# A four-layer graph network on one core: the last norm of six batches on another path, and the first loads in another order

## The chip, the cores and the metric

The kernel runs on one core of a Trainium2 chip. The metric is the device time of one execution in microseconds, from the runs shown below; lower is better. A profile of one execution goes with it. In the profile PE is TensorE's matmul, PEld its weight load, DVE is VectorE, ACT is ScalarE, POOL is GpSimd, and SP is the engine that issues most DMAs.

## What is computed

The input x has 64 batches of 256 nodes with 128 channels, all float32, and one adjacency matrix adj of 256 x 256 is shared by all batches. Four layers follow one another, each of the form x = layernorm(x + f(x)):

```python
def _layernorm(x, axis=-1, eps=1e-5):
    m = jnp.mean(x, axis=axis, keepdims=True)
    v = jnp.var(x, axis=axis, keepdims=True)
    return (x - m) / jnp.sqrt(v + eps)
...
x = _layernorm(x + _L0_gnn_ref(x, adj, adj, L0_gnn_weight_1), axis=-1)
x = _layernorm(x + _L1_gnn_ref(x, adj, L1_gnn_weight, L1_gnn_bias), axis=-1)
x = _layernorm(x + _L2_gnn_ref(x, adj, L2_gnn_W, L2_gnn_b), axis=-1)
x = _layernorm(x + _L3_gnn_ref(x, adj, adj, L3_gnn_w3_w, ...), axis=-1)
```

Layer 0 propagates x up to three times through adj, with a weight of 128 x 128 for each of seven terms. Layers 1 and 2 propagate once and multiply by one weight. Layer 3 is a gated unit that runs five steps on a state h:

```python
def step(h, _):
    m_in = jnp.einsum('nm,bmd->bnd', in_matrix, h)
    m_out = jnp.einsum('nm,bmd->bnd', out_matrix, h)
    av = jnp.concatenate([m_in, m_out], axis=-1)
    u3 = h @ u3_w.T + u3_b
    z = jax.nn.sigmoid(av @ w3_w.T + w3_b + u3)
    r = jax.nn.sigmoid(av @ w4_w.T + w4_b + u3)
    hv = jnp.tanh(av @ w5_w.T + w5_b + (r * h @ u5_w.T + u5_b))
    h = (1.0 - z) * h + z * hv
    return (h, None)
```

## The kernel before

The 64 batches are worked off in 32 groups of two batches. A group's state is a tile of 128 x 512: two batches times two halves of the nodes, each 128 x 128 and called a q. At most ten groups are in work at once (ACTIVE).

**The order is planned.** The kernel's code does not issue anything directly. Each operation is recorded with an engine, an estimated cost, a lag until its result is seen, and a rank (Plan.add, L61). Plan.order (L84) then simulates the engines with these estimates: at each step it takes the operation that can start earliest, and among those that can start equally early the one with the lowest rank, then the one recorded first. The result is one list, and each engine works off its part of it strictly in order, waiting for whatever the real data needs. The argument `after` of an operation delays it in the plan only. Buffers are slots in pools ("bank" for the eight PSUM banks, "w" for general 128 x 512 tiles in SBUF and so on; L203), and the plan takes into account when a slot comes free.

**Ranks.** Operations of the preamble have ranks written out by hand in calls of `pre`, `fetch` and `load`. A group's operations have the number of the group as rank. Only for the last seven groups (LEVEL) is it different: there each group lies 0.1 above the one before it, and each operation 0.02 above the group's preceding one (Group.rank, L454), so that these groups advance side by side. The load of x of a group has the group's rank less 1.5.

**The preamble** (L232 to L412). POOL builds the identity matrix, TensorE makes 14 transposes of it to warm up (WARM), and SP loads adj (a_nat), x of the first two groups, layer 0's weight w0 (448 KB; w_raw in the profile), then w1 and six raw weights of layers 2 and 3. POOL loads the biases: b1 and b2, spread over all partitions, into two of the three parts of a tile wb (w1 is the third), and six small ones into braw. TensorE transposes adj and squares it. VectorE makes the degree sums of adj (degree, L325), of which POOL takes the power -1/2 (dinv, L342). VectorE makes the sums of w0's parts (w0_sums, L286) and subtracts each row's mean (centre, L295), and does the same to wb (L375), so that layers 0 to 2 deliver results whose mean over the channels is zero already. It forms four sets of block sums of the adjacency matrices (block_sums, L350), with which `propagate` needs seven block products in place of eight. `less` (L386) is the identity with 1/128 subtracted everywhere, that is I - 1/C. The function `transposed` (L389) turns the raw weights on TensorE.

**Layer 3 and the end of a group** (L795 to L827). Layer 3 works on the transposed state hT, with the channels on the partitions. A step propagates h, and makes the products pr and ph in PSUM, from which ScalarE makes r, z and hv; VectorE makes rh, d = hv - hT, e = z*d and the new hT = hT + e. After the last step the result must be turned back, added to y, which is the result of layer 2, and normalised:

- In all groups but the last two, hT is turned back by a VectorE transpose of 32 x 32 blocks and two passes through DRAM (`turned`, `brought`: one DMA out, four back). Then VectorE makes s = hn + y (residual, L539) and its statistics (L480: bn_stats, bn_aggr, variance + eps, negated mean), POOL the power -1/2 and the product with the mean, and ScalarE the scaled and shifted result (L549).
- In the last two groups (END = 4 batches, from batch 60 on), VectorE writes hT in another order, TensorE transposes it (`transposes`, pth, L659), VectorE adds y from there and makes statistics, POOL makes the power, and VectorE itself makes the result (near, L552).

In layers 0 to 2 the sum has the mean zero by construction, so `spread_of` (L507) needs only the squares, which ScalarE sums with accum_out; POOL adds eps and takes the power -1/2.

Of the kernel before, what the change touches and what calls it, by code (L numbers as in the profile page):

```python
# [10 lines left out]
OP = mybir.AluOpType  # L11
# [7 lines left out]
PLAIN = 0  # L19
END = 4  # L20
STEPS = 5
WARM = 14
ONES = (0, 0)
# [134 lines left out]
def kernel(  # L158
# [39 lines left out]
    def mm(o, lhsT, rhs, start, stop, shared=False):  # L198
# [3 lines left out]
              "ve": [P, Q], "rs": [P, Q]}  # L202
    slots = {"bank": BANKS, "x": ACTIVE + 3, "w": 64, "th": 10, "q": 10, "dram1": 8, "dram2": 16, "st": 12, "mv": 12, "ve": 24, "rs": 12}  # L203
    plan = Plan(slots)
# [9 lines left out]

    def pre(rank, engine, cost, run, reads=(), writes=(), lag=None, joint=False):
        lag = lag or {"SP": 2300, "PE": 260, "DVE": 260, "ACT": 130, "POOL": 100}[engine]
        plan.add(engine, cost, lag, rank, run, reads, writes, joint=joint)


    QUEUES = {"SP": (nc.sync, 450), "ACT": (nc.scalar, 450), "POOL": (nc.gpsimd, 1000)}  # L220

    def fetch(rank, o, src, v, queue):
        e, cost = QUEUES[queue]
        pre(rank, queue, cost, lambda: e.dma_start(o, src), [], [v], lag=3000, joint=True)

# [55 lines left out]

    w0_raw = load(0.01, "w0_raw", [P, C, K0], w0)

# [86 lines left out]

    wb, wbm = constant("wb", [P, 3, C]), constant("wbm", [P, 3])
    fetch(0.1, wb.ap[:, 0, :], w1, wb, "SP")
    for i, b in ((1, b1), (2, b2)):
        fetch(0.1, wb.ap[:, i, :], bass.AP(tensor=b.tensor, offset=b.offset, ap=[[0, P], [1, C]]), wb, "POOL")
    pre(0.35, "DVE", 1100, lambda: centre(wb, wbm), [wb], [wb, wbm])  # L375
    w1c, b1c, b2c = ((wb, wb.ap[:, i, :]) for i in range(3))
    raw = {name: load(0.1, f"raw_{name}", [P, src.shape[1]], src, False, "SP")
           for name, src in (("w2", w2), ("w4", w4_w), ("w3", w3_w), ("w5", w5_w), ("u3", u3_w), ("u5", u5_w))}
# [10 lines left out]
    def transposed(name, *parts_):  # L389
        ps, v = temp(f"p_{name}"), constant(name, [P, len(parts_) * P])  # L390

        def run():
            for i, src in enumerate(parts_):
                if src is raw["w2"]:
                    mm(ps.ap[:, i * P:(i + 1) * P], src.ap, less.ap, True, True)
                else:
                    nc.tensor.transpose(ps.ap[:, i * P:(i + 1) * P], src.ap, ident)

        n = len(parts_) * P
        pre(0.4, "PE", len(parts_) * 110, run, [*parts_, less], [ps])  # L400
        pre(0.4, "ACT", act_cost(n), lambda: nc.scalar.copy(v.ap, ps.ap[:, :n]), [ps], [v])
        return [(v, v.ap[:, i * P:(i + 1) * P]) for i in range(len(parts_))]
# [6 lines left out]
    for i, src in enumerate((w3_b, w4_b, w5_b, u3_b, u3_b, u5_b)):  # L409
        fetch(0.2, braw.ap[:, i:i + 1], src.rearrange("(p o) -> p o", o=1), braw, "POOL")  # L410
    pre(0.4, "DVE", 150, lambda: nc.vector.tensor_add(bsum.ap, braw.ap[:, :3], braw.ap[:, 3:]), [braw], [bsum])
# [26 lines left out]
    class Group:  # L438
        def __init__(self, start, nb):
# [3 lines left out]
            self.q, self.width = nb * T, nb * N  # L443

        def view(self, ap):
            return ap[self.start:self.start + self.nb].rearrange("b (t p) c -> p (b t) c", p=P)
# [11 lines left out]
        def add(self, engine, cost, lag, run, reads=(), writes=(), joint=False, behind=()):  # L458
            after = behind if self.first else self.gate
            self.count += 1  # L460
            op = plan.add(engine, cost, lag, self.rank(), run, reads, writes, after, joint)
            self.first = self.first or op
            self.last = op
            return op
# [14 lines left out]

        def statistics(self, tag, s, near):  # L480
            st, mv, ve, rs, nm = (self.val(k, n + tag) for k, n in (
                ("st", "st"), ("mv", "mv"), ("ve", "ve"), ("rs", "rs"), ("ve", "nm")))
            kept = () if near else (nm,)

            def stats():
                for q in range(self.q):
                    nc.vector.bn_stats(st.ap[:, q * 6:(q + 1) * 6], nat(s)[:, q, :])  # L487

            def aggr():
                for q in range(self.q):  # L490
                    nc.vector.bn_aggr(mv.ap[:, 2 * q:2 * q + 2], st.ap[:, q * 6:(q + 1) * 6])
                mean, var = (mv.ap.rearrange("p (q k) -> p k q", k=2)[:, k] for k in range(2))
                nc.vector.tensor_scalar(ve.ap, var, EPS, None, op0=OP.add)
                if not near:
                    nc.vector.tensor_scalar(nm.ap, mean, -1.0, None, op0=OP.mult)

            def scales():
                nc.gpsimd.tensor_tensor(rs.ap, ve.ap, half[:, :self.q], op=OP.pow)
                if not near:
                    nc.gpsimd.tensor_tensor(mv.ap[:, :self.q], nm.ap, rs.ap, op=OP.mult)  # L500

            self.dve(stats, [s], [st], 195 * self.q)
            self.dve(aggr, [st], [mv, ve, *kept], 67 * self.q + (142 if near else 240))
            self.add("POOL", 1010 if near else 1300, 100, scales, [ve, *kept], [rs] if near else [rs, mv])
            return mv, rs
# [33 lines left out]
        def residual(self, tag, ps, resid, left=lambda v: v.ap, right=lambda v: v.ap):  # L539
            s = self.val("w", "s" + tag)  # L540
            self.dve(lambda: nc.vector.tensor_add(right(s), left(ps), right(resid)), [ps, resid], [s])  # L541
            return (s, *self.statistics(tag, s, self.start >= B - END))

        def normalise(self, tag, s, mv, rs):
# [6 lines left out]

            def near():  # L552
                for q in range(self.q):
                    nc.vector.tensor_scalar(nat(y)[:, q, :], nat(s)[:, q, :], mv.ap[:, 2 * q:2 * q + 1],  # L554
                                            rs.ap[:, q:q + 1], op0=OP.subtract, op1=OP.mult)

            if self.start >= B - END:
                self.dve(near, [s, mv, rs], [y], 257 * self.q)
            else:
                self.act(run, [s, mv, rs], [y], 390 * self.q)  # L560
            return y

# [154 lines left out]
        def record(self):  # L717
# [80 lines left out]
            for s in range(STEPS):  # L798
# [3 lines left out]
                self.product(pr, u3T, hT, False, True)  # L802
                r = self.gate_(f"r{s}", pr, AF.Sigmoid, rb)
                rh = self.tensor(f"rh{s}", OP.mult, r, hT)
                ph = self.val("bank", f"ph{s}")
# [5 lines left out]

                d = self.tensor(f"d{s}", OP.subtract, hv, hT)
                e = self.tensor(f"e{s}", OP.mult, z, d, into=pr)
                if s < STEPS - 1:
# [7 lines left out]
            else:  # L822
                hT = self.tensor("hT", OP.add, hT, e, lambda v: v.ap.rearrange("p (k q i) -> p q k i", k=4, q=self.q),
                                 lambda v: v.ap.rearrange("p (q k i) -> p q k i", k=4, q=self.q))
                last = self.residual("3", self.transposes("h", hT), y)
            o = self.normalise("3", *last)
# [67 lines left out]
```

## Time and profile before

| | |
|---|---|
| median of 7 runs | 1358.71 us (1356.84 to 1359.73) |
| the profiled execution's own time | 1358.96 us |
| its span, first to last instruction | 1357.2 us |
| TensorE busy | 1332.8 us, 98% of the span |
| VectorE, ScalarE, POOL busy | 954.1, 755.9, 675.5 us |
| granted TensorE clock, mean | 0.995 of full speed |
| load of w_raw, issue to landing | 7.5 us, issued at 2.27 us |
| last product of layer 3 starts | 1339.04 us |
| last VectorE instruction ends | 1353.19 us |

The page gives busy times by engine, a line of digits for the granted clock in 40 slices, and groups of instructions. The chain of waits follows the execution back from its end, at each step to what released it. Timeline lines give the start, the duration, the engine, the line of the kernel, the operation and its tiles, and in brackets how long the engine was idle before and what ended that. Names are those of the tiles, without the numbers at their ends, so w0_raw is w_raw. A matmul in float32 of 128 x 128 by 128 x 512 is two records; a transpose is one.

### The profile page before, as it was taken

To read this page: it belongs to the slowest core of one execution; us is meant where nothing else is said; L and a number is where in the kernel's file an instruction comes from. 1 tells how busy PE (TensorE), PEld (TensorE's weight loads), DVE (VectorE), ACT (ScalarE), POOL (GpSimd) and SP (SyncE) were. 2 spreads that over 40 slices of the span, in tenths; PEclk is the share of its full clock that TensorE was granted. 3 is DMA by queue.
4 is the path that set the end of the run, shared out by engine and by line. 5 is a ranking of instruction groups with operands and counts; after the bars stand their busy time and mean duration, and the time that the engine had idled before them with its cause. 6 is when DMAs were issued, how large, how long until landed. Compare 5 with 4: busy or idle time off the path is not lost.

```text
span 1357.2 us, 21892 instructions
## 1 busy us (share of the span) xinstructions
PE 1332.8 (98%) x6509; PEld 923.8 (68%) x6509; DVE 954.1 (70%) x2343; ACT 755.9 (56%) x2398; POOL 675.5 (50%) x1095
## 2 busy tenths in 40 slices
PE   8999999999999999999999999999999999999995
PEld 7986666766776776776676667766776776556552
DVE  5356678778667677677767767766565778777778
ACT  4666464665456565657455466554655686444444
POOL 5786343654446544547354455543744685232322
PEclk9999999999999999999999999999999999999998
DMA  6322333433333322434243333332432233333333
GB/s 172 103 63 63 99 96 104 138 109 116 94 102 95 109 72 85 125 109 125 61 126 110 101 102 109 99 99 68 117 94 63 71 102 119 92 101 93 93 91 104
DMA packets 270214, 135.47 MB, mean 100 GB/s; under 512 B 175856, under 2 KB 241648, under 8 KB 270096
## 3 DMA queue, kind: packets, MB, share of 16 engines
q1 hardware_dynamic: 269840, 133.95, 34.0%
q8 instruction: 52, 0.85, 0.3%
q14 instruction: 66, 0.54, 0.1%
q0 software_dynamic: 256, 0.13, 0.1%
HBM read 67.57 MB, written 66.06 MB: 98 GB/s over the span
## 4 chain that ended last, share of the span: by engine, by line
PE 94%; DVE 3%; DMA 1%; issue 1%; ACT 0%; SPq 0%; POOL 0%; POOLq 0%; DVEq 0%; ACTq 0%
PE pr L199 30%; PE ph L199 20%; PE pmg L199 18%; PE py L199 16%; PE pm L199 7%; PE pmq L199 3%; DMA x<-in_x_dram 1%; DMA w_raw<-in_L_gnn_weight_dram 1%; DVE st L487 0%; DVE s L541 0%; DVE rh L714 0%; ACT y L529 0%; DVE y L554 0%; DVE d L714 0%; DVE hT L714 0%
## 5 line engine op out<-in xcount | busy, mean ns | idle before, releaser
L199 PE MATMUL pr<-mg,w435u5T 128*128 128x512 f32 x640 | 320.2, 593 | 0.8 <-ACT r L707 0.8
L599 POOL TENSOR_TENSOR tsg<-h 128x256 f32<-128x256 f32 x128 | 95.2, 743 | 212.1 <-DMA h<-dh 153.8
L707 ACT ACTIVATE r<-pr,bsum 128x512 f32<-128x512 f32 x160 | 109.7, 686 | 151.2 <-PE pr L199 149.6
L714 DVE TENSOR_TENSOR rh<-r,hT 128x512 f32<-128x512 f32 x160 | 126.8, 794 | 71.7 <-ACT r L707 67.5
L707 ACT ACTIVATE pr<-pr,bsum 128x512 f32<-128x512 f32 x160 | 105.6, 660 | 120.7 <-PE pr L199 116.0
L199 PE MATMUL ph<-rh,w435u5T 128*128 128x512 f32 x320 | 164.1, 596 | 0.8 <-DVE rh L714 0.7
L714 DVE TENSOR_TENSOR d<-ph,hT 128x512 f32<-128x512 f32 x160 | 109.8, 686 | 78.0 <-ACT ph L707 77.0
L199 PE MATMUL ph<-mg,w435u5T 128*128 128x512 f32 x320 | 163.4, 593 | 0.0
L199 PE MATMUL pr<-hT,w2u3T 128*128 128x512 f32 x320 | 162.2, 593 | 0.0
L199 PEld LDWEIGHTS pr<-mg,w435u5T 128*128 128x128 f32 x640 | 109.0, 191 | 64.8 <-issue 48.8
L707 ACT ACTIVATE ph<-ph,bsum 128x512 f32<-128x512 f32 x160 | 105.5, 659 | 63.6 <-PE ph L199 63.4
L529 ACT ACTIVATE y<-s,rs 128x128 f32<-128x128 f32 x384 | 122.1, 392 | 15.2 <-POOL rs L518 14.4
L517 POOL TENSOR_SCALAR ve<-ve 128x4 f32<-128x4 f32 x96 | 22.3, 232 | 214.3 <-ACT y L513 214.2
L199 PEld LDWEIGHTS pmg<-s_aTp,tsg 128*128 128x128 f32 x768 | 102.1, 191 | 34.6 <-issue 29.8
L513 ACT ACTIVATE y<-s 128x128 f32<-128x128 f32 x384 | 113.7, 300 | 18.4 <-DVE s L536 18.2
L199 PEld LDWEIGHTS pmg<-aTp,h 128*128 128x128 f32 x512 | 88.0, 197 | 46.8 <-issue 35.4
L714 DVE TENSOR_TENSOR pr<-pr,d 128x512 f32<-128x512 f32 x160 | 110.6, 692 | 1.5
L714 DVE TENSOR_TENSOR hT<-hT,pr 128x512 f32<-128x512 f32 x160 | 108.6, 680 | 1.7
L627 DVE TENSOR_TENSOR usg<-usg,pmg 128x128 f32<-128x128 f32 x160 | 45.2, 284 | 90.9 <-PE pmg L199 67.1
L199 PE MATMUL pmg<-s_aTp,tsg 128*128 128x128 f32 x768 | 106.4, 275 | 0.0
L637 DVE TENSOR_TENSOR mg<-pmg,usg 128x256 f32<-128x256 f32 x160 | 67.1, 420 | 51.9 <-PE pmg L199 50.1
L518 POOL TENSOR_TENSOR rs<-ve,half 128x4 f32<-128x4 f32 x96 | 99.5, 1037 | 8.0
(175 smaller groups left out, 2808.4 us busy)
## 6 DMA issues: line engine op xcount, KB each, us to landing
dh<-th SPq DMA_DIRECT2D x160, 256.0 KB, 2.0
h<-dh SPq DMA_DIRECT2D x256, 128.0 KB, 2.5
x<-in_x_dram SPq DMA_DIRECT2D x32, 256.0 KB, 3.3
hT<-dh SPq DMA_DIRECT2D x128, 64.0 KB, 2.0
out_dram<-y SPq DMA_DIRECT2D x32, 256.0 KB, 2.3
dx<-tx SPq DMA_DIRECT2D x30, 256.0 KB, 2.7
xT<-dx SPq DMA_DIRECT2D x60, 128.0 KB, 2.6
dn<-tn SPq DMA_DIRECT2D x30, 256.0 KB, 2.0
```

The source lines that it names most:

```text
L199: nc.tensor.matmul(o, lhsT, rhs, start=start, stop=stop, skip_group_check=shared)
L513: nc.scalar.activation(nat(y)[:, q, :], nat(s)[:, q, :], AF.Square, scale=C ** -0.5, accum_out=ve.ap[:, q:q + 1])
L517: nc.gpsimd.tensor_scalar(ve.ap, ve.ap, EPS, None, op0=OP.add)
L518: nc.gpsimd.tensor_tensor(rs.ap, ve.ap, half[:, :self.q], op=OP.pow)
L529: nc.scalar.mul(nat(y)[:, q, :], nat(s)[:, q, :], rs.ap[:, q:q + 1])
L599: nc.gpsimd.tensor_tensor(ts.ap[:, :2 * P].rearrange("p (x c) -> p x c", x=2), ins(h)[:, 1], ins(h)[:, :, 0], op=OP.subtract)
L627: nc.vector.tensor_tensor(row(u, 0), row(u, 1), row(ps, 3), op=OP.add)
L637: nc.vector.tensor_tensor(o(m, slice(1, 3)), o(ps, slice(1, 3), False), both, op=OP.add)
L707: self.act(lambda: nc.scalar.activation(t.ap, ps.ap, func, bias=bias[1], scale=1.0), [ps, bias[0]], [t], act_cost(self.width) + 100)
L714: self.dve(lambda: nc.vector.tensor_tensor(out(t), way(a), way(b), op=op), [a, b], [t])
```

## The change

**Layer 3's norm, in the last six batches** (END = 6, so three groups in place of two). The old path of those groups is gone, and with it the cases for `near` in `statistics` and `normalise`. The sum y + h + e is now formed by TensorE in one PSUM bank: hT before the last update, copied by ScalarE into another order (hc), is multiplied by `less`, y by the identity, and e by `less`. A product of the transposed tile with I - 1/C turns it back and subtracts the mean in one; y has the mean zero already. The first two products may run before the last step's e is known; they are held back in the plan until the gate r of the last step. Then ScalarE sums squares, POOL makes the power -1/2, and VectorE multiplies by it. The last hT = hT + e is not formed in these groups.

**The head.** A new copy on VectorE (`made`) writes a few values of the identity into the part of wb that the bias loads overwrite, so that these must wait for it. The six small bias loads are planned after the last of them has landed. w0's load has the rank -1 in place of 0.01, between those of x of the first and the second group. w1 and the raw weights have 0.6 in place of 0.1, the centring of wb 0.9 in place of 0.35, after w0s, and the transposes of the raw weights 2.1 in place of 0.4. There are 12 warming transposes in place of 14, and 48 buffers of kind w in place of 64.

```diff
-END = 4
+END = 6
-WARM = 14
+WARM = 12
...
-    slots = {"bank": BANKS, "x": ACTIVE + 3, "w": 64, ...
+    slots = {"bank": BANKS, "x": ACTIVE + 3, "w": 48, ...
...
-    w0_raw = load(0.01, "w0_raw", [P, C, K0], w0)
+    w0_raw = load(-1, "w0_raw", [P, C, K0], w0)
...
-    fetch(0.1, wb.ap[:, 0, :], w1, wb, "SP")
+
+    made = pre(-9, "DVE", 100, lambda: nc.vector.tensor_copy(wb.ap[:, 1:3, 0], ident[:, :2]), [], [wb])
+    fetch(0.6, wb.ap[:, 0, :], w1, wb, "SP")
     for i, b in ((1, b1), (2, b2)):
-        fetch(0.1, wb.ap[:, i, :], bass.AP(...), wb, "POOL")
-    pre(0.35, "DVE", 1100, lambda: centre(wb, wbm), [wb], [wb, wbm])
+        last = fetch(0.1, wb.ap[:, i, :], bass.AP(...), wb, "POOL", (made,))
+    pre(0.9, "DVE", 1100, lambda: centre(wb, wbm), [wb, w0s], [wb, wbm])
-    raw = {name: load(0.1, f"raw_{name}", [P, src.shape[1]], src, False, "SP")
+    raw = {name: load(0.6, f"raw_{name}", [P, src.shape[1]], src, False, "SP")
...
-        pre(0.4, "PE", len(parts_) * 110, run, [*parts_, less], [ps])
-        pre(0.4, "ACT", act_cost(n), lambda: nc.scalar.copy(v.ap, ps.ap[:, :n]), [ps], [v])
+        pre(2.1, "PE", len(parts_) * 110, run, [*parts_, less], [ps])
+        pre(2.1, "ACT", act_cost(n), lambda: nc.scalar.copy(v.ap, ps.ap[:, :n]), [ps], [v])
...
-        fetch(0.2, braw.ap[:, i:i + 1], src.rearrange("(p o) -> p o", o=1), braw, "POOL")
+        fetch(0.2, braw.ap[:, i:i + 1], src.rearrange("(p o) -> p o", o=1), braw, "POOL", (last,))
...
+        def closing(self, y, hT, e, behind):
+            s, hc = self.val("bank", "s3"), self.val("w", "hc")
+            way, out_ = self.by_tile
+            self.act(lambda: nc.scalar.copy(out_(hc), way(hT)), [hT], [hc])
+
+            def turned(v, start, stop):
+                for q in range(self.q):
+                    mm(s.ap[:, q * P:(q + 1) * P], v.ap[:, q * P:(q + 1) * P], less.ap, start and q == 0, stop, shared=True)
+
+            def early():
+                turned(hc, True, False)
+                mm(s.ap, ident, y.ap, False, False, shared=True)
+
+            self.pe(pe_cost(P, self.q) + pe_cost(self.width), early, [hc, y, less], [s], behind=(behind,))
+            self.pe(pe_cost(P, self.q), lambda: turned(e, False, True), [e, less], [s])
+            o, rs = self.spread_of("3", s)
+            self.dve(lambda: nc.vector.tensor_tensor(nat(o), nat(s), rs.ap[:, :, None].to_broadcast([P, self.q, C]),
+                                                     op=OP.mult), [s, rs], [o])
+            return o
...
                 r = self.gate_(f"r{s}", pr, AF.Sigmoid, rb)
+                gated = self.last
...
                 d = self.tensor(f"d{s}", OP.subtract, hv, hT)
+                if s == STEPS - 1 and self.start >= B - END:
+                    e = self.tensor("e", OP.mult, z, d, *self.by_tile)
+                    break
                 e = self.tensor(f"e{s}", OP.mult, z, d, into=pr)
...
             else:
-                hT = self.tensor("hT", OP.add, hT, e, ...)
-                last = self.residual("3", self.transposes("h", hT), y)
+                o = self.closing(y, hT, e, gated)
+                self.add("SP", 450, 2700, lambda: nc.sync.dma_start(self.view(out), nat(o)), [o], [])
+                return
```

## The prediction

> **What bounds the kernel now.** I read the page first: the busy table and the slices.
>
> ```profile
> PE 1332.8 (98%) x6509; PEld 923.8 (68%) x6509; DVE 954.1 (70%) x2343; ACT 755.9 (56%) x2398; POOL 675.5 (50%) x1095
> ...
> PEclk9999999999999999999999999999999999999998
> ```
>
> TensorE is busy in 98% of the span, at full clock. By the windows it is idle for about 2.2 us in all between 40 and 1330 us. So only three things can move the time: how early this saturated stretch starts, how much work is put into it, and how long the tail behind it is. For the start I read the chain of waits of the first 60 us.
>
> ```profile
> 2.27 7.54 DMA w_raw<-in_L_gnn_weight_dram
> 9.84 0.39 DVE w0s L287
> ...
> 21.73 0.63 DVE tx L730
> ...
> 29.43 4.71 DMA x<-in_x_dram
> 34.28 0.68 PE pmq L199 x4
> ```
>
> See what leads to what: layer 0's weight w_raw lands at 9.8 us, VectorE works off the whole preamble in one unbroken run until it comes to tx at 21.7, tx releases the stores and, queued behind them on SP, the next loads of x, and TensorE stands until x is there at 34.28. Before w_raw, VectorE sits idle 4.57 us. For the end I read the windows (columns: busy of PE, PEld, DVE, ACT, POOL, then clock, DMA) and the timeline.
>
> ```profile
> 1330.00:1340.00 10.00, 9.00 (x23) 3.44 (x21) 9.37 (x31) 5.44 (x10) 2.89 (x4) 1.00 0.40 127
> 1340.00:1350.00 10.00, 1.94 (x9) 1.13 (x8) 9.83 (x43) 3.84 (x9) 3.35 (x5) 0.80 0.34 97
> ```
>
> ```profile
> 1339.04 1.13 PE L199 MATMUL ph<-rh,w435u5T 128*128 128x512 f32 x2 [0.23 <-DVE rh L714]
> ...
> 1341.72 0.63 ACT L707 ACTIVATE ph<-ph,bsum 128x512 f32<-128x512 f32 x1
> ...
> 1343.67 0.67 DVE L714 TENSOR_TENSOR d<-ph,hT 128x512 f32<-128x512 f32 x1
> ...
> 1344.74 0.69 DVE L714 TENSOR_TENSOR pr<-pr,d 128x512 f32<-128x512 f32 x1
> ...
> 1348.89 0.69 DVE L541 TENSOR_TENSOR s<-pth,y 128x512 f32<-128x512 f32 x1
> ...
> 1352.08 1.11 DVE L554 TENSOR_SCALAR y<-s,mv,rs 128x128 f32<-128x128 f32 x4 [1.12 <-POOL rs L498]
> ```
>
> The last product of the last group starts at 1339.04. From there to the end of its y at 1353.19 there are 14.15 us, and VectorE, 98% busy between 1340 and 1350, is what the group waits for: tanh ends at 1342.35, and d starts only at 1343.67, e at 1344.74, s at 1348.89. In 1330 to 1340 TensorE is still nearly full; the holes the timeline names late in it are 0.78 us (until r of the last group, 1337.69) and 0.23 us (before the line shown).
>
> **What the Trainium skill says here.** "DMA: Bandwidth & Descriptors", Queues, rings and completion order: within one ring descriptors are consumed in order, and a DMA engine takes turns between queues. The trace agrees: the rate falls from 299 GB/s (3 to 4 us) to 153 and 175 GB/s (4 to 6 us) while POOL's bias loads are in flight beside SP's queue. "Perfetto Trace Analysis", Transposes: transposes skip the arithmetic and should not be ordinary matmuls. Here four transposes of pth are four records, while each 128x128 product is two; the change replaces the former by the latter. "ScalarE: Activation LUTs", What ACT_TABLE_LOAD costs: an ACTIVATE with immediate scale takes 186 ns plus 0.833 ns per element, 293 ns for 128; the trace has 298 for the squares at L513. "TensorE: Matmul & The Clock Gate", Part 1: half clock after an idle window; the 0.80 in the window from 1340 agrees.
>
> **Part 1, the head.** *w_raw goes ahead of the second load of x.* 256 KB leave its way; at the 182 GB/s that moved in the window from 0 to 10 us, that is 1.4 us. That it is issued at 1.73 in place of 2.27 is part of those 1.4, not more. *The identity.* Now POOL starts a bias load at 1.28 ahead of the identity's second half (2.15 to 2.46). With the new copy into wb the two bias loads must wait for the identity, so they start about 0.7 us later (identity done near 1.3, copy and hand-off to about 2.0), and six tiny bias loads go behind dinv. Behind the bias loads' new wait on POOL stands only dinv, whose sums end at 5.27: 0. That is a further small relief for w_raw: at least 0, at most some 2 us (half rate for 4 to 6 us, plus what follows); I take 0.3. So w_raw lands near 8.1, 1.7 us earlier. *Centring of wb (1.29 us from 11.03) goes behind w0s.* VectorE's sum stays the same; w0s is ready earlier, which TensorE can use for groups 0 and 1, but it then only waits longer for x at 34.28: 0. If that wait were gone, it would be worth up to the 1.6 us that p_w2u3T now waits on raw weights (0.36 and 1.24). *Two warming transposes fewer* (0.2 us each) and the earlier identity: adjacency ready about 1.5 us sooner, 0 for the same reason. *Raw weights, w1, transposes to later ranks*: SP still has nothing else ready, so I keep their issue times; the transposes (0.9 us of TensorE) only move later, and layers 2 and 3, which use them, start after 40 us: 0. They set a limit: the last lands near 12.5 (where TensorE's wait for raw_u ends), and VectorE reads the group at 14.36. VectorE's run can move forward by at most about 1.9 us before it waits there. Moving 1.7 gives no new wait, and tx, the stores, the x loads and 34.28 all follow. **Head: -1.7**, from 0 to -3.5.
>
> **Part 2, the middle.** Buffers of kind w fall from 64 to 48, and the whole order is computed anew. No row shows a wait for these buffers. Bounds: -2.2 (all idle time between 40 and 1330 gone) to +2 (as much again); I take 0.
>
> **Part 3, the tail, per group of two batches, now three groups.** Removed from VectorE in each of the last two: hT 0.69, s 0.68, four stats 0.87, aggregates 0.37, ve 0.17, y 1.11 = 3.89. Added: o, a 512-wide tensor_tensor from PSUM, 0.69 by the row of d. The third from last loses hT, transpose, s, stats, aggregates, ve and nm, 3.6, for 0.69, and five DMAs on SP. VectorE sheds 3.2 + 3.2 + 2.9 = 9.3 of the 21.2 us it is busy after 1330, and stops being the tail's bound.
>
> Next is the chain of the last group, from its last product: product 1.13, tanh 0.66, d 0.69, e 0.69, four 128x128 products of e (8 records at 0.11 and 0.2 to finish) 1.1, four squares 1.28 (24.43 to 25.71 in group 0), POOL's add and pow 1.35 (26.63 to 27.98), o 0.69, six hand-offs of 0.05: 7.9 us in place of 14.15, **6.25 less**. Squares from PSUM are not shown before; copies of 128 from PSUM at L640 take 0.27, so I see no surcharge (up to 0.2).
>
> But TensorE pays. Four products of h (0.89) and the identity product of y (0.86) are 1.75 per group, products of e 0.89 more: 2.64 against the 0.44 of the transposes. For the groups before the last this comes where TensorE is full. Their ranks: each group lies 0.1 apart, each operation adds 0.02, so the third-last group's closing (2.64) stands ahead of the last group's w5 and later products, and the second-last's (2.64) is tied with the last one. I count 2 x 2.64 = 5.3 ahead of the last product, less the holes of 0.78 and 0.23 and a little of the wait for r at 1331.9 (0.4): **+3.9**. The last group's own 1.75 fits between its last product and e (0.66 + 0.69 + 0.69 with hand-offs: 2.2), nobody waits; if not, it costs up to 1.75. ScalarE's three copies hc (0.59) run before, beside products: 0; y of an older group (1.65) stood ahead of tanh at 1340.16, but with the product 3.9 later it is done. **Tail: -6.25 + 3.9 = -2.3**, from +1 to -5.
>
> **Sum.** -1.7 - 2.3 = -4.0. The profiled run took 1358.96 with a span of 1357.2; less 4.0 it is 1354.96, and the median lies 0.25 under that run: **1354.7 us**.
>
> **Rivals.** *Covers hold:* TensorE's closing work falls into waits for r and rh, only 1.75 of it ahead of the last product (tail -4.5), and w_raw is clear of the bias loads, with the raw weights landing earlier too (head -3.0): -7.5, 1351.2. For it: 4.57 us of idle VectorE before w_raw; against: the raw weights at 12.5. *Given back:* raw weights or x land as late as now (head 0) and the tail keeps 1.0: 1357.7. The change not doing what it says comes to this: were the bias loads not held by the identity, only 1.4 of the head would stay. *Slower, TensorE pays for the tail:* the last group's own 1.75 is also queued ahead of its last product: 7.1 us of matmuls with no hole filled, last product at 1346.1, then tanh behind a 1.65 us normalisation and the pow behind another's 1.35: 7.1 + 3.0 - 6.25 = +3.9, with the head +2.2: 1360.9. It decides where added matmuls and queueing exceed 6.25 + 1.7 = 7.95 us. For it: 9.00 of 10 busy; against: holes exist and ranks put the last closing last.
>
> **Chances.** Forecast 0.50 (own range 1352.5 to 1356.8), covers hold 0.24, given back 0.14, slower 0.12. Range: 1350.4 to 1358.4, which cuts the far halves of the first and the last rival. A measurement here can tell about 0.2% (2.7 us) from none: faster 0.72 (most of the forecast and the first rival), same 0.17, slower 0.11.
>
> **What would show it.** w_raw landing near 8.1, tx at about 20.0, the wait on x ending near 32.6 instead of 34.28; the last ph<-rh product about 2.2 us later than now (1341.2, head included); from its start to the end of o about 7.9 us; o about 0.69. Wrong if VectorE still queues d or e for over 1 us, if tx does not move, or if TensorE's idle time between 40 and 1330 grows beyond 4 us.

## The result and the profile after

The changed kernel takes 1354.27 us (median of 14 runs, 1350.91 to 1355.53), the kernel before, measured beside it, 1358.68 us (34 runs, 1356.39 to 1360.19). The ratio is 0.9967, with a 95% interval of 0.9960 to 0.9974: about 4.5 us faster. The profiled execution of the changed kernel took 1354.07 us with a span of 1352.1, 5.1 less than the 1357.2 of before.

The busy table and the slices of the page after:

```profile
PE 1336.5 (99%) x6553; PEld 928.4 (69%) x6553; DVE 942.2 (70%) x2304; ACT 758.0 (56%) x2421; POOL 679.8 (50%) x1097
...
PEclk9999999999999999999999999999999999999999
```

TensorE has 44 records more and is 3.7 us longer busy, VectorE has 39 instructions fewer and is 11.9 us less busy. The span still is TensorE's.

The start, in the chain that ended last (start, duration, what):

```profile
1.74 8.34 DMA w_raw<-in_L_gnn_weight_dram
...
10.10 0.38 DVE w0s L287
...
36.15 4.32 DMA x<-in_x_dram
40.49 0.71 DVE tx L745
```

w_raw is issued 0.53 us earlier than before (1.74 in place of 2.27), but it takes 8.34 us in place of 7.54, and lands 0.27 later, at 10.08. VectorE's timeline shows the rest:

```profile
10.10 0.38 DVE L287 TENSOR_TENSOR w0s<-w_raw,ident 128x128 f32<-128x128 f32 x1 [4.83 <-DMA w_raw<-in_L_gnn_weight_dram]
...
22.53 0.71 DVE L745 STREAM_TRANSPOSE tx<-x 128x512 f32<-128x512 f32 x1
```

It still stands 4.83 us idle before w_raw (before: 4.57), and tx comes at 22.53, where the chain of before had it at 21.73. So w_raw is neither there earlier nor is tx. How much of the 0.27 and the 0.8 is chance can't be told from one execution each: the run with the tail alone below has the head of the kernel before, and in its profile w_raw takes 8.21 us and lands at 10.49.

The end, first by windows (busy of PE, PEld, DVE, ACT, POOL, then clock, DMA share, GB/s):

```profile
1330.00:1340.00 10.00, 10.00 (x45) 6.18 (x45) 7.66 (x23) 7.55 (x21) 4.35 (x6) 1.00 0.31 91
1340.00:1350.00 10.00, 5.23 (x30) 3.60 (x29) 4.68 (x15) 5.13 (x22) 3.73 (x6) 0.95 0.41 117
```

VectorE's 9.83 of the second window has become 4.68, and TensorE's hole in the first (9.00) is full. Then the timeline of the last group:

```profile
1340.67 1.02 PE L199 MATMUL ph<-rh,w435u5T 128*128 128x512 f32 x2
...
1341.73 0.66 ACT L722 ACTIVATE ph<-ph,bsum 128x512 f32<-128x512 f32 x1 [0.20 <-PE ph L199]
...
1342.43 0.69 DVE L729 TENSOR_TENSOR d<-ph,hT 128x512 f32<-128x512 f32 x1 [0.48 <-ACT ph L722]
...
1343.15 0.69 DVE L729 TENSOR_TENSOR e<-pr,d 128x512 f32<-128x512 f32 x1
...
1344.18 1.05 PE L199 MATMUL s<-less,e 128*128 128x128 f32 x8
...
1345.33 0.28 ACT L515 ACTIVATE y<-s 128x128 f32<-128x128 f32 x1
...
1346.87 1.04 POOL L520 TENSOR_TENSOR rs<-ve,half 128x4 f32<-128x4 f32 x1
...
1347.94 0.69 DVE L574 TENSOR_TENSOR y<-s,rs 128x512 f32<-128x512 f32 x1 [2.01 <-POOL rs L520]
```

d starts 0.04 us behind the end of tanh (before: 1.32), e follows at once, and the last VectorE instruction ends at 1348.63. From the start of the last product that is 7.96 us, before it was 14.15.

The 5.1 us of span, taken apart in the two profiled executions (one of each kernel): everything ahead of the tail stands 1.15 us earlier (the r of one and the same late step, in a stretch that TensorE works off in the same order, starts at 1325.22 in place of 1326.37); the last product comes 1.63 later all the same, so 2.78 of matmuls were put ahead of it; the chain behind it is 6.19 shorter; and from the last VectorE instruction to the end of the span there are 3.47 in place of 4.01. -1.15 + 2.78 - 6.19 - 0.54 = -5.1.

### The profile page after: what moved, and what is told of

Same layout as the page of the kernel before. It is cut to its first block, busy times and chain, and to the rows that moved or that the text cites. A ratio compares the mean times of both kernels' runs of the same rounds, so it can differ in the third digit from the quotient of the medians.

```text
span 1352.1 us, 22012 instructions
## 1 busy us (share of the span) xinstructions
PE 1336.5 (99%) x6553; PEld 928.4 (69%) x6553; DVE 942.2 (70%) x2304; ACT 758.0 (56%) x2421; POOL 679.8 (50%) x1097
## 4 chain that ended last, share of the span: by engine, by line
PE 97%; DMA 1%; DVE 1%; ACT 1%; issue 0%; SPq 0%; POOLq 0%; ACTq 0%; POOL 0%; DVEq 0%
PE pr L199 30%; PE ph L199 20%; PE pmg L199 19%; PE py L199 16%; PE pm L199 7%; PE pmq L199 4%; DMA w_raw<-in_L_gnn_weight_dram 1%; PE s L199 0%; DMA dx<-tx 0%; DMA x<-in_x_dram 0%; ACT y L515 0%; ACT y L551 0%; DVE s L543 0%; PE p_an L259 0%; POOLq L908 0%
## 5 line engine op out<-in xcount | busy, mean ns | idle before, releaser
L729 DVE TENSOR_TENSOR rh<-r,hT 128x512 f32<-128x512 f32 x160 | 123.4, 772 | 61.7 <-ACT r L722 60.9
L515 ACT ACTIVATE y<-s 128x128 f32<-128x128 f32 x396 | 116.7, 299 | 17.0 <-DVE s L538 15.0
L520 POOL TENSOR_TENSOR rs<-ve,half 128x4 f32<-128x4 f32 x99 | 103.5, 1045 | 8.3
```

The lines of the kernel that those rows point to most:

```text
L515: nc.scalar.activation(nat(y)[:, q, :], nat(s)[:, q, :], AF.Square, scale=C ** -0.5, accum_out=ve.ap[:, q:q + 1])
L729: self.dve(lambda: nc.vector.tensor_tensor(out(t), way(a), way(b), op=op), [a, b], [t])
```

## The experiments

From the two traces my theory was that the tail brings nearly all and the head nothing, because the bias loads hold w_raw up; the rivals put the gain in the head, or in a new order of the middle. The expectations name theories by letters and say in words what each stands for. In the table below, "ahead" means this: TensorE's matmul records up to a given time are counted by shape and weighted with their spacing in the trace (0.1115, 0.2145 and 0.4295 us for 128, 256 and 512 columns), and the same sum of the kernel before is taken away. The warming transposes are left out.

**The tail alone.** The kernel before's head, buffers and loads, with the changed closing of the last three groups:

```diff
-WARM = 12
+WARM = 14
-"w": 48
+"w": 64
-    w0_raw = load(-1, "w0_raw", [P, C, K0], w0)
+    w0_raw = load(0.01, "w0_raw", [P, C, K0], w0)
...
```

> The closing on TensorE for the last six batches alone; the head, the ranks and the 64 buffers are those of the kernel before, and up to the tail every engine works in the order of before. Theory S (the tail carries most): the last product starts some 2.8 us later than before, its chain to the end takes 7.9 to 8.0 us in place of 14.15, so the time falls by 3.4 to 4.0 us. Theory P (the prediction's sum): the product is 3.9 us later and the time falls by 2.3. Theory H (the head carries most): it falls by less than 1.5.

Measured: 1354.98 us, ratio 0.9974 (0.9964 to 0.9985), about -3.5 us. The last product and the last VectorE instruction of its profile:

```profile
1341.74 1.02 PE L199 MATMUL ph<-rh,w435u5T 128*128 128x512 f32 x2
...
1348.95 0.69 DVE L573 TENSOR_TENSOR y<-s,rs 128x512 f32<-128x512 f32 x1 [1.95 <-POOL rs L519]
```

The last product starts 2.70 us later than before, with no lead from the head. That is the price of the added matmuls, measured without the head. The chain behind it takes 7.90 us, so theory S holds in all its parts.

**The head alone.** The kernel before with all edits of loads, ranks, warming and buffers, and its old norms.

```diff
-    w0_raw = load(0.01, "w0_raw", [P, C, K0], w0)
+    w0_raw = load(-1, "w0_raw", [P, C, K0], w0)
...
+    made = pre(-9, "DVE", 100, lambda: nc.vector.tensor_copy(wb.ap[:, 1:3, 0], ident[:, :2]), [], [wb])
...
```

> The head, the ranks and the 48 buffers of the changed kernel with the old tail (two groups, norm by VectorE). Theory S: w_raw still lands near 10 us, the x transposes tx are later than before, and what is gained comes from less waiting between 60 and 1330: 0.7 to 1.3 us less than before. Theory P: 1.7 less, with tx near 20. Theory N (the head is no gain at all): within 0.5 of before.

Measured: 1358.30 us, ratio 0.9995 (0.9987 to 1.0003): no gain that can be measured. Its chain shows the reason again:

```profile
1.73 8.47 DMA w_raw<-in_L_gnn_weight_dram
...
36.72 4.87 DMA x<-in_x_dram
41.61 0.71 DVE tx L731
```

w_raw lands at 10.2, no earlier than with the old head (9.81 and 10.49 in the two profiles that have it), and tx comes at 22.66. The ratio says -0.7 us, the medians -0.3, so theories S and N are not told apart; theory P's 1.7 lies at the edge of the interval, and its tx near 20 did not come. The parts add up: -0.7 and -3.5 against -4.5 of the whole, with intervals that reach 1 us and more to either side.

**Two groups in place of three.**

```diff
-END = 6
+END = 4
```

> The changed kernel with the closing in the last two groups only (END = 4); the third-last goes through DRAM and VectorE as before. If TensorE's closing work of that group (1.75 + 0.89 us) is what holds up the last product, this is 0.5 to 2 us faster than the changed kernel. If VectorE's 3.6 us and the DRAM passes of that group are what the third closing was worth taking away, it is 0.5 to 3 us slower, and a normalisation on ScalarE ends last.

Measured: 1356.13 us, ratio 0.9983 (0.9976 to 0.9989), 1.9 us more than with three groups. The last group's o ends at 1348.79 here, but it is no longer what ends last. ScalarE's timeline:

```profile
1349.36 1.65 ACT L551 ACTIVATE y<-s,mv,rs 128x128 f32<-128x128 f32 x4 [2.73 <-POOL mv L502]
```

The third-last group goes back through DMA and VectorE's statistics, and its y ends at 1351.01. So with two groups the old path of the third-last group ends last, and the third group's closing is needed.

**The bias loads behind w_raw.** The copy that the two loads wait for reads w_raw, so they start when it has landed; the planner is told, and draws up a new order.

```diff
-    made = pre(-9, "DVE", 100, lambda: nc.vector.tensor_copy(wb.ap[:, 1:3, 0], ident[:, :2]), [], [wb])
+    made = pre(-9, "DVE", 100, lambda: nc.vector.tensor_copy(wb.ap[:, 1:3, 0], w0_raw.ap[:, :2, 0]), [w0_raw], [wb])
```

> The changed kernel, in which the copy that holds back POOL's two bias loads reads w_raw in place of the identity, so that these loads start only when w_raw has landed. Theory B (w_raw lands late since these two loads stop the DMA engines that it still needs): w_raw lands before 7.5 us in place of 10.1, the sums of w0 start 2.5 us earlier. If the head then decides the start of the saturated stretch, the time falls by 1 to 2.5 us more; if raw weights and x do, by less than 0.7. Rival Q (the queue's own bytes decide): w_raw still lands after 9 us.

Measured: 1355.99 us, ratio 0.9980 (0.9974 to 0.9987), slower than the changed kernel, though the loads did what the theory said. Its chain:

```profile
1.73 5.58 DMA w_raw<-in_L_gnn_weight_dram
...
19.41 0.73 DVE tx L745
```

w_raw lands 2.8 us earlier and tx comes 3.1 earlier than in the changed kernel. At 60 us TensorE is 2.4 us ahead of before, at 1200 us it is 1.1 behind. The loads do hold w_raw up, but the time that I expected from it did not come, and a new question came up: was the lead lost because a gain at the head is always given back, or because this kernel has another order of the middle? The next two runs put this in a square: loads held or not, order of the changed kernel or the new one.

**Held, in the order of the changed kernel.** The planner sees the old dependences; the loads are issued out of the step that computes dinv.

```diff
+    def inverse():
+        nc.gpsimd.tensor_tensor(dinv.ap, deg.ap, half[:, :T], op=OP.pow)
+        nc.vector.tensor_copy(wb.ap[:, 1:3, 0], w0_raw.ap[:, :2, 0])
+        for issue in held:
+            issue()
...
-    pre(0.3, "POOL", 700, lambda: nc.gpsimd.tensor_tensor(dinv.ap, deg.ap, half[:, :T], op=OP.pow), [deg], [dinv])
+    pre(0.3, "POOL", 700, inverse, [deg], [dinv])
```

> The changed kernel with its own order of work on every engine; only GpSimd's two loads of the biases now stand behind its inverse root of the degrees, and wait until w_raw has landed. Theory O (the earlier w_raw is worth what it moves, and the other kernel with this hold lost it to another order of the middle): w_raw lands near 7.4, tx at 20.0 or earlier (in the changed kernel 22.5), TensorE is some 2.0 to 2.4 us ahead of the changed kernel from 60 us to the end, nothing is lost between 1090 and 1130 us, last product near 1338.5, time 1351.9 (1351.2 to 1352.8). Rival G (whatever is won at the head is given back to waits in the middle, in any order): tx at 20.0 too, but the lead shrinks to under 0.7 us before 1300 us, time 1353.6 to 1356.

**The new order, loads early.** The planner sees the dependence on w_raw; the loads are issued right behind the identity.

```diff
-    made = pre(-9, "DVE", 100, lambda: nc.vector.tensor_copy(wb.ap[:, 1:3, 0], ident[:, :2]), [], [wb])
+    made = pre(-9, "DVE", 100, lambda: None, [w0_raw], [wb])
...
+    def lessened():
+        nc.vector.tensor_copy(wb.ap[:, 1:3, 0], ident[:, :2])
+        for issue in held:
+            issue()
...
```

> The order of work of the kernel that holds the bias loads until w_raw has landed, with the loads themselves issued early again, as in the changed kernel: the order of the middle alone. Theory O: w_raw lands near 10, tx at 22.5, and TensorE loses some 2.5 to 3.5 us between 1090 and 1130 us against the changed kernel: time 1357.4 (1356.5 to 1358.5). Rival G: an order as good as the other, time 1354.3 within 0.7.

Measured, with how far TensorE is ahead of the kernel before (us). The rows come from three batches of runs, each with its own runs of the kernel before (medians 1358.68, 1358.13 and 1358.56):

```
                            time us   ratio to before           60    400   1000   1200   1320
changed (early, its order)  1354.27   0.9967 (0.9960-0.9974)   +0.3   +0.7   +1.0   +1.3   +1.1
held, its order             1351.12   0.9948 (0.9934-0.9961)   +4.5   +5.1   +5.1   +5.2   +5.2
held, new order             1355.99   0.9980 (0.9974-0.9987)   +2.4   +1.5   +1.5   -1.1   -1.1
early, new order            1358.96   1.0006 (0.9998-1.0014)   +0.3   -0.8   -0.6   -3.2   -3.2
```

Both effects are there, each in both rows: holding the loads is worth about 3 us (3.15 and 2.97 by the medians, 2.6 and 3.5 by the ratios), the new order costs about 5 (4.7 and 4.9 by the medians, 5.3 and 4.3 by the ratios). Theory O is right about what happens and G is refuted: what is won at the head stays to the last product. O's sizes were too small: it put the lead of the held kernel over the changed one at 2.0 to 2.4 us, and it is 3.9 to 4.4; it put the new order with early loads at 1356.5 to 1358.5 us, and it took 1358.96. (The profiled execution of the held kernel took 1349.90 us, the least of its five, so its lead is larger than its gain in the medians.) In the chain of the held kernel

```profile
1.74 5.23 DMA w_raw<-in_L_gnn_weight_dram
...
31.84 4.38 DMA x<-in_x_dram
36.24 0.71 DVE tx L754
```

the load of x that ends at the tx of 36.24 begins 4.3 us earlier than the one at 36.15 in the changed kernel. That is more than the 3.1 us by which w_raw lands earlier. The granted clock may be part of it, since the chain of the changed kernel runs through TensorE there. From 12 to 14 us, first in the changed kernel, then in the held one (the clock is the third number from the end):

```profile
12.00:14.00 2.00, 2.00 (x10) 1.91 (x10) 1.93 (x5) 0.27 (x1) 0.00 (x0) 0.50 0.42 105
```

```profile
12.00:14.00 2.00, 2.00 (x11) 1.77 (x10) 1.94 (x10) 0.85 (x2) 1.15 (x3) 1.00 0.49 125
```

In the changed kernel TensorE waits 3.9 us for ahat, which VectorE scales only behind w_raw, and then works at half clock until some 14.5 us; in the held kernel that wait is 0.5 us and the clock stays full. The wait alone doesn't decide it: in the run with early loads and the new order it is 3.2 us, and the clock stays at 1.00. There the 24 matmuls behind the wait (p_an, ptx, pmq) take 4.53 us, in the changed kernel 5.75, so the half clock costs 1.2 us. In how many executions of each kernel it comes isn't on record. The place where the new order loses most shows in a window of it, here of the run with early loads, and after it of the held kernel in its own order:

```profile
1090.00:1130.00 40.00, 37.63 (x262) 31.42 (x261) 29.43 (x83) 31.56 (x151) 34.05 (x52) 1.00 0.31 93
```

```profile
1090.00:1130.00 40.00, 39.57 (x229) 29.21 (x230) 28.52 (x73) 31.99 (x134) 33.54 (x54) 1.00 0.35 107
```

and in the waits of that window of the run with early loads (waited for: us, times, longest):

```profile
PE pmg L199 <- ACT usg L664: 1.1, 2, 0.6
PE pmg L199 <- ACT y L524: 0.8, 1, 0.8
```

Propagations of layer 3 stand in TensorE's queue ahead of the ScalarE copies and norms that feed them. 1.9 us of the 2.6 that are lost between 1000 and 1200 us are these waits; another 1.1 go between 60 and 400 us, where TensorE's idle time is 0.5 us in all, and for those no wait is named. In the rows with held loads 2.1 are missing at 60 us already. The waits show where this order loses; why the planner's estimates led to it wasn't tried.

**The head alone, with the loads held.** The kernel with the head alone and the same edit as in the held kernel.

> The kernel before with the head of the change, and in it the two bias loads behind w_raw; norms of layer 3 as before; every engine's order is that of the run with the head of the change alone, but for those two loads and the copy ahead of them. Theory B (the early bias loads stop w_raw, and that is why the head alone gave nothing): w_raw lands near 7.0, tx near 19.3, TensorE 3.5 to 4.3 us ahead of the head alone all the way, last product near 1335.5, time 1355.0 (1354.3 to 1355.9), 3.3 less than the head alone. Rival A (the held version gained only together with the new tail): 1357 to 1358.5.

Measured: 1354.42 us, ratio 0.9968 (0.9957 to 0.9980).

```profile
1.74 5.15 DMA w_raw<-in_L_gnn_weight_dram
...
1333.67 1.12 PE L199 MATMUL ph<-rh,w435u5T 128*128 128x512 f32 x2 [0.23 <-DVE rh L724]
```

w_raw lands at 6.89, tx comes at 19.19, the last product starts 1.8 us earlier than theory B had it. The head alone gave nothing, with the loads out of the way it gives as much as the whole change: theory B, and the bias loads are the cause. The tail of before on top of it still costs about 3 us against the held kernel (1351.12). Of the head alone, two of 13 executions took 1354.51 and 1354.52 us, near the held version, and of the changed kernel two of 14 took 1350.91 and 1351.73, near the held kernel; no trace of these four was kept, so what differed in them is open.

**Which property of those loads?** First the loads went to ScalarE's queue, behind the copy from the identity:

```diff
+    def mark():
+        nc.vector.tensor_copy(wb.ap[:, 1:3, 0], ident[:, :2])
+        for i, b in ((1, b1), (2, b2)):
+            nc.scalar.dma_start(wb.ap[:, i, :], bass.AP(...))
```

> The changed kernel with the two bias loads issued by ScalarE's queue instead of GpSimd's, at about the same time (behind the copy from the identity and the table load, some 2.2 us); all else in its order. Theory Q (it is the loads through GpSimd's queue[...] that hold w_raw up): w_raw lands at 7.0 to 8.3, tx at 19.3 to 20.5, time 1351.3 (1350.5 to 1352.5). Rival E (any load of 128 KB there that goes to all partitions from one row holds w_raw up): w_raw lands at 9.3 to 10.3, tx at 22 to 22.8, time 1354.3 within 0.8.

Measured: 1354.94 us, ratio 0.9974 (0.9964 to 0.9983). This run didn't test what it should. ScalarE's timeline:

```profile
8.40 0.38 ACTq L376 DMA_DIRECT2D wb<-in_L_gnn_bias_dram  x1
8.82 0.44 ACTq L376 DMA_DIRECT2D wb<-in_L_gnn_b_dram  x1
9.30 0.58 ACT L270 COPY aT<-p_at 128x512 f32<-128x512 f32 x1 [7.08 <-DVE ahat L334]
```

The copy that they wait for was done by 1.5 us, but they were issued only at 8.4, and what held them until then isn't shown. aT stood behind them, so TensorE waited 4.1 us for aT. VectorE had w_raw at 7.59, since the loads were held again. The question of the queue stayed open.

Then from ScalarE's queue with no wait, out of the step with the first activation:

```diff
+    def first():
+        nc.scalar.activation(early.ap, half, AF.Sigmoid)
+        for issue in held:
+            issue()
```

> The changed kernel with the two bias loads issued by ScalarE's queue right behind its table load, at 2.2 us and with no wait; all else in its order. Theory Q (it is GpSimd's queue that makes these loads hold w_raw up): w_raw lands at 7.0 to 8.3, tx at 19.3 to 20.5, time 1351.3 (1350.5 to 1352.5). Rival E (any load there that goes to all partitions from one row holds w_raw up, whatever queue issues it): w_raw lands at 9.3 to 10.3, tx at 22 to 22.8, time 1354.3 within 0.8.

Measured: 1353.55 us, ratio 0.9963 (0.9950 to 0.9977).

```profile
1.74 7.30 DMA w_raw<-in_L_gnn_weight_dram
```

The loads were issued at 0.91 and 1.33, beside the table load and not behind it as I had expected, so the first stands ahead of x and both ahead of w_raw; the adjacency took 3.8 us in place of 2.8, and w_raw landed at 9.04. This lies between the two theories, with the loads in another place: from ScalarE's queue they don't free w_raw either, but they delay it in another way. The packed trace has every DMA packet, and those of 3584 bytes are w_raw's alone. Here the first of them starts at 5.29 us, in the changed kernel at 3.60; from there to the end of the last it is 3.3 us, in the changed kernel 6.1. So w_raw starts late and is not drawn out: ahead of it on SP's queue stand the adjacency, itself 1.0 us late, and x.

Last, GpSimd's queue, in the old place, with w1's 128 rows taken twice in place of the one row of b1 and of b2 for all partitions (the biases of layers 1 and 2 are left out):

```diff
-        last = fetch(0.1, wb.ap[:, i, :], bass.AP(tensor=b.tensor, offset=b.offset, ap=[[0, P], [1, C]]), wb, "POOL", (made,))
+        last = fetch(0.1, wb.ap[:, i, :], w1, wb, "POOL", (made,))
```

> The changed kernel with GpSimd's two early loads taking w1 row by row (128 rows of 512 bytes) instead of b1 and b2 for all partitions: the two biases are left out of the result. Same bytes, same queue, same place. Theory Q (the queue): w_raw lands at 9.3 to 10.3, time 1354.3 within 1. Rival E (the one row for all partitions): w_raw lands at 7.0 to 8.3, tx at 19.3 to 20.5, time 1351.3 (1350.3 to 1352.7).

Measured: 1352.05 us, ratio 0.9953 (0.9939 to 0.9966).

```profile
1.73 6.25 DMA w_raw<-in_L_gnn_weight_dram
```

w_raw lands at 7.98 and tx comes at 20.47. GpSimd's queue in the first 24 us (packets, MB, share of 16 engines), first in the changed kernel, then here:

```profile
q0 software_dynamic: 256, 0.13, 7.5%
```

```profile
q0 software_dynamic: 256, 0.13, 2.3%
```

The 256 packets hold the six tiny loads of braw too, which are the same in both. The packets of this queue take 28.8 us of the DMA engines' time (0.075 x 16 x 24) when the two loads come from one row each, and 8.8 us when they come from 128; the two loads themselves are 32 packets of 4096 bytes, which take 26.2 and 6.4 us. w_raw takes 8.34, 6.25, or 5.23 when the loads are held: about 2.1 of the 3.1 us are the one row, 1.0 the load as such. These are single executions; in the five profiles with this head and early bias loads w_raw takes 8.34 to 8.76. On GpSimd's queue, then, rival E holds for most of it. The engines' time fits in direction, not in size: spread evenly over 16 engines, 20 us are 1.25 us of each (an estimate from these figures), and w_raw gains 2.1. And the one row isn't slow by itself: from ScalarE's queue the same two loads took 1.9% in packets of 512 bytes. Why one row is slow on GpSimd's queue wasn't tried.

**Less work for TensorE ahead of the last product.** Closing by TensorE for the last two groups; the third-last with VectorE's norm, as before had it for its last two; the last group's early matmuls behind its last product.

```diff
+CLOSE = 4
...
-                if s == STEPS - 1 and self.start >= B - END:
+                if s == STEPS - 1 and self.start >= B - CLOSE:
...
+                if self.start == B - NB:
+                    gated = self.last
```

> The changed kernel with the closing by TensorE for the last two groups only; the third last group's norm goes back to VectorE, as the kernel before had it for its last two, and the last group's early matmuls wait for its last product. Theory T (the added matmuls ahead of the last product are the price): 1.75 + 0.89 less 0.44 of transposes and up to 1 us of holes, last product 1.2 to 2.2 us earlier than 1340.67, the same 7.96 us behind it, time 1352.5 (1352.0 to 1353.2). Rival V (the VectorE work that the change takes away is worth as much: four statistics, their aggregates and four y stand ahead of the last rh, d and e): rh, d or e of the last group wait for VectorE 1 us or more, time 1353.8 to 1356.

Measured: 1355.37 us, ratio 0.9976 (0.9967 to 0.9985), 1.1 us more than the changed kernel, with intervals that overlap; what is sure is that it isn't the 1352.5 of theory T. Its timeline:

```profile
1339.94 1.13 PE L200 MATMUL ph<-rh,w435u5T 128*128 128x512 f32 x2
...
1340.62 1.64 ACT L555 ACTIVATE y<-s,mv,rs 128x128 f32<-128x128 f32 x4
...
1342.16 0.64 ACT L734 ACTIVATE ph<-ph,bsum 128x512 f32<-128x512 f32 x1
1342.38 1.10 DVE L560 TENSOR_SCALAR y<-s,mv,rs 128x128 f32<-128x128 f32 x4
...
1343.95 0.68 DVE L741 TENSOR_TENSOR d<-ph,hT 128x512 f32<-128x512 f32 x1
```

The last product comes earlier, by 0.73 and, since this execution was 1.0 us behind at 1320, by 1.7 in the tail: theory T has the size of the matmuls right. But tanh starts 1.2 us later behind it than in the changed kernel, behind an older group's y on ScalarE, and d stands 1.15 us behind VectorE's old work. The chain is 10.25 us in place of 7.96. Rival V wins: the work that comes back to VectorE and ScalarE costs the chain 2.3 us, more than the 1.7 that TensorE is spared.

## Why the prediction was right, and where it was not

The predicted time, 1354.7, is 0.4 us from the median, but by luck: two of its three terms were wrong, and they cancelled. The head was to bring 1.7 and brought nothing measurable when made alone, the tail was to bring 2.3 and brought 3.5. One of the prediction's own signs of being wrong came true: tx did not move forward.

*Head, "-1.7": failed, in its mechanism.* Two steps failed. "256 KB leave its way ... that is 1.4 us" came true for w_raw's start only: its first packet starts at 3.60 us in place of 4.69. The step left the stretch from its first packet to its last as it was, and that grew from 4.7 to 6.1 us; with the loads held it is 2.9. The second step, "a further small relief for w_raw: at least 0", took it that bias loads which start later (0.7 us by the prediction, 0.53 and 0.18 measured) hold w_raw up less. Their packets run from 4.36 to 9.22 us in place of 3.54 to 7.60, and w_raw's now from 3.60 to 9.72: the two overlap for 4.9 us in place of 2.9. The two together brought nothing: w_raw lands at 10.1 to 10.5 in the five profiles with the new head and early bias loads, at 9.8 and 10.5 in the two with the old one. The falling rate that the prediction itself quoted was the sign: between 4 and 6 us before moves 153 and 175 GB/s, the held kernel 268 and 332. It fits what the Trainium skill says in "DMA: Bandwidth & Descriptors", Issuing engines are not separate DMA queues: loads of all engines run on the same 16 DMA engines and interleave. The runs agree: from ScalarE's queue the loads held w_raw up too (7.30 against 5.23 us). The way from w_raw on was right: with the loads held, tx and the load of x stand 3.3 and 4.3 us ahead of the changed kernel's, and the time is 3.15 less. The limit of "at most about 1.9 us" from the raw weights did not hold: the held kernel's VectorE reads that group of raw weights at 11.10 in place of 14.36 without a wait, because they came earlier too (SP was through with issuing them at 7.3 us, in the kernel before at 9.0). What moving w_raw ahead of x is worth without the other edits wasn't run.

*Middle, 0 within -2.2 to +2: right for this change.* The head alone, whose order of the middle is that of the changed kernel, neither won nor lost. With 64 buffers of kind w the planner writes the very same order, so that edit changes nothing in it. But the bounds were too narrow for what a new order can do: another one cost 4.7 us.

*Tail, chain "7.9 us in place of 14.15": right.* It is 7.96. The products of e took 1.05 us for 1.1, the squares 1.14 for 1.28, POOL's two steps 1.35 for 1.35; at the squares ScalarE came free from an older y at 1345.29, 0.06 us after the products ended, so there was no slack left.

*Tail, "+3.9" of TensorE's work: mis-sized.* 2.70 in the tail alone, 2.78 in the changed kernel. The prediction put both other groups' closing, 5.28, ahead of the last product. The second-last group's products of e stand behind it (1341.53), so 4.39 stand ahead. The holes that they filled are then 1.6 us, and the gaps in the timeline of before between 1331 and the last product come to 1.6 as well; the prediction counted 1.4. The tie that it named was decided the other way. The last group's own 1.75 fitted between product and e as predicted, but for some 0.3 us: the products of e start 0.34 us behind e, in the run with two groups, where TensorE stood idle, 0.06. It costs nearly nothing, since ScalarE wasn't free for the squares before.

*The end behind the chain* (-0.54) was not in the prediction.

*The rivals.* "Covers hold" named the bias loads and the raw weights, at 1351.2 with w_raw clear of the bias loads. The changed kernel is not that. The held kernel has the number, 1351.12, and the head, but not the tail of that rival: 4.39 us of closing and not 1.75 stand ahead of its last product. "Given back" had the right head (0) but kept too little of the tail. "TensorE pays" did not come: the matmuls were less than half of the 6.2 that the chain lost.

## What to carry to other kernels

A small load can be a long one: look up in the trace how much of the DMA engines' time a load takes that runs beside another, and don't price it by its bytes alone. In this kernel it paid to let a load through GpSimd's queue that fetches one row for all partitions wait until the load that everybody waits for had landed. When a plan computes the order, an edit is two changes, the edit and a new order; hold the order fixed to see what the edit is worth, since here the order alone moved 4 to 5 us. And a total that comes out right proves no term of it: measure the parts alone.

## What the runs showed of the hardware that was not expected

- 128 KB fetched as one row of 512 bytes for all 128 partitions, by two loads through GpSimd's queue, took 26.2 us of DMA-engine time in 32 packets of 4096 bytes; as 128 rows, also in 32 packets, 6.4 us. The load of 448 KB beside them took 8.34 and 6.25 us, and 5.23 without them.
- The two one-row loads issued by ScalarE in the first 1.8 us, 128 KB in 288 packets, took 1.9% of the engines' first 24 us, or 7.3 us, a quarter of the above, and w_raw still took 7.30 us, since it started later. So the engine time of the packets doesn't explain all of it, and the rest is open.
- In the changed kernel a wait of TensorE of 3.9 us behind w_raw came with half clock right after it, and the 24 matmuls there took 5.75 us in place of 4.53 at full clock. In the held kernel, with a wait of 0.5 us, the clock stayed full.
